# Strassen's rule in the output projection, another product order in the second MLP layer, and operand sums formed earlier

## The chip, the cores and the metric

The kernel runs on one core of one Trainium2 chip. The metric is the device time of one execution in microseconds (us), median of three runs. In this text TensorE multiplies matrices, VectorE (DVE in the profile) and GpSimd (POOL) do elementwise arithmetic, ScalarE (ACT) does activations and copies, and SyncE (SP) starts most transfers. SBUF is the on-chip memory, PSUM the memory that TensorE writes its results to.

## The reference

The input is x, 2 images of 512 channels by 32 x 32 points, in fp32. Two layers follow each other.

The first is a deformable attention block: batch norm, grouped query, offsets from a strided depthwise convolution, keys and values sampled at 64 shifted points, a bias from a small network on all pairs of positions (by far the longest part), softmax, and then the part that this study is about:

```python
out = einsum('bchw,oc->bohw', out, out_w) + out_b     # output projection, 512 x 512
x = x + out
h1 = gelu(einsum(bn2(x), mlp_w1) + mlp_b1)            # MLP, 512 -> 2048
x = x + einsum(h1, mlp_w2) + mlp_b2                   # MLP, 2048 -> 512
```

The second is a full self-attention over the 1024 points of each image, with 512 channels:

```python
attn = softmax((xt @ Wq.T + bq) @ (xt @ Wk.T + bk).T / sqrt(512))
x = x + (attn @ (xt @ Wv.T + bv)) @ Wp.T + bp
```

All products are in fp32.

## The kernel before

**Stages.** The attention bias is computed in 256 slices, up to about 2040 us. Then come, without a barrier, the output projection, the MLP, and the self-attention of image 0 and of image 1. xs holds the running x of both images in SBUF; the projection adds to it, the MLP adds to it, and the self-attention adds to it and stores it.

**Products by Strassen's rule.** Both MLP layers and all of the self-attention multiply 2 x 2 blocks with seven block products in place of eight (the Winograd form, with operand sums that are shared). A block of the moving operand is 128 partitions x 2 x 512. `fold` makes the three weight sums and changes a fourth block in place (four operations, on GpSimd for weights that come from memory). `spread` does the same with the moving operand on VectorE (lines 601, 602, 603 and 605: sums 4 and 5, block 1 in place, sum 6). `PARTS` says which weight block meets which moving block:

```python
PARTS = {1: (0, 0), 2: (1, 2), 3: (6, 3), 4: (2, 6), 5: (4, 4), 6: (5, 5), 7: (3, 1)}
```

So products 1, 2 and 3 need no sum of the moving operand, 5 needs sum 4, 6 needs sum 5, 7 needs block 1 after its change, and 4 needs sum 6. `multiply(pool, order, product, took)` takes the products in a given order: it gets a PSUM tile of two banks, issues four matmuls of 128 x 128 by 512, and calls `took[p]`, which reads the tile on VectorE (`plus`) or ScalarE (copy). In the MLP and the self-attention the PSUM pool mq has four such tiles, so the fifth product waits until the first has been read. In the projection the pool is zp, with three.

**Output projection** (`project(b, h)`, line 657): plain. Four calls, by image and half of the points; in each, four output chunks of four matmuls, 64 matmuls in all. After each chunk VectorE adds it and the bias to xs (line 661). Weights are in vp (already multiplied with the values), the moving operand is qa, the softmax result. The last softmax (`tail`: transpose `pt`, line 533; sums; two transposes `pb`, line 551, that ScalarE copies into qa) runs during image 0's projection and is needed by image 1's.

**MLP.** Eight units: image b, and p of 0 to 3, a quarter of the hidden width. In a unit `layer1` forms a hidden block hm, with GELU on ScalarE (line 690); then `spread(hm)`; then `layer2` multiplies it with the second weights, products in the order 3, 2, 7, 1, 5, 6, 4. Products 2, 3 and 4 are added straight to xs (`give`); 1, 5, 6 and 7 are summed over the four units in acc (`own`), which the last unit adds into xs. `normalise(b)` writes xb, the MLP's input, on ScalarE; `spread(xb)` follows. `load_unit` loads the two weight blocks of the next unit (line 636) and folds them on GpSimd (line 598); there are two buffers of each.

**Self-attention.** `blocks(b)` forms the operand sums of xs on VectorE (tx, lines 793 to 796), and uc is a small sum of a bias. `multiply` then forms the queries (product order 1, 6, 7, 4, 5, 3, 2), the scores, the values and the result.

**What sets the order.** Each engine works through its own queue in order. A tile layer puts in the semaphore waits and fixes each queue's order when the program is built, so an operation can stand elsewhere than in the text. A tile that takes the place of an older one in SBUF or PSUM waits until the older one has been read. The tiles of the MLP's pool mp lie where tiles of the bias stage were.

## Time and profile before

| | |
|---|---|
| time, median of 3 runs | 2813.57 us (2812.54 to 2814.28) |
| span of the profiled execution | 2814.2 us |
| output projection | about 2040.6 to 2098.0 us |
| MLP, eight units | 2098.0 to 2495.6 us |
| self-attention | from 2495.6 us |

The profile gives times within one execution. Its lines of groups and of the timeline read: start (in the timeline), busy us, engine, line of the kernel, operation, output <- inputs, shapes, count, and in brackets the idle time of the engine just before, with what ended it. In the list of stretches each engine has its busy time; the number after the five engines is the TensorE clock that was granted, as a share of full speed. An fp32 matmul of this kernel appears as two records.

### The profile page before, as it was taken

The page shows a single profiled execution, that of the slowest core. Times are in us where ns is not written, and L with a number is a line of the kernel's source. Part 1 is how long each engine was busy: PE and PEld are TensorE (multiplying, and loading weights), DVE is VectorE, ACT ScalarE, POOL GpSimd, SP SyncE. Part 2 cuts the span into 40 slices and gives each one's busy share as a digit, 9 for nine tenths or more (in the row PEclk, how much of TensorE's full clock was granted, in tenths as well). Part 3 has the DMA queues.
Part 4 walks back from the last instruction along what each step waited for, and adds up shares of the span by engine and source line. Part 5 has one row for each costly group of instructions (what it writes and reads, how often), then busy time and mean ns, then how long its engine had stood idle before and what let it go on. Part 6 is the DMA issues. An engine that isn't in the chain of part 4 may idle for free. (4 is left out here: it accounts for less than half of the span.)

```text
span 2814.2 us, 46282 instructions
## 1 busy us (share of the span) xinstructions
PE 2766.7 (98%) x20162; PEld 994.4 (35%) x20162; DVE 2252.5 (80%) x1472; ACT 1562.5 (56%) x1584; POOL 349.7 (12%) x418
## 2 busy tenths in 40 slices
PE   9999999999999999999999999999999999989999
PEld 3332322332233233333333333333344444436455
DVE  5899999899989999899999999999734464365454
ACT  4667667766776677666667667667612031114131
POOL 2111111111110111111111111111132222000000
PEclk9999999999999999999999999999999999999999
DMA  4444344434443444444444444444331101000000
GB/s 166 94 83 99 76 86 89 98 76 83 83 107 68 83 84 83 91 88 86 94 88 86 96 85 91 89 91 83 68 135 45 40 35 45 15 15 1 30 1 30
DMA packets 63530, 210.10 MB, mean 75 GB/s; under 512 B 10976, under 2 KB 13536, under 8 KB 60640
## 3 DMA queue, kind: packets, MB, share of 16 engines
q0 software_dynamic: 36864, 135.28, 25.1%
q1 hardware_dynamic: 25600, 70.79, 8.4%
q8 instruction: 159, 2.61, 0.4%
q10 hardware_dynamic: 864, 1.07, 0.1%
q14 instruction: 43, 0.35, 0.0%
HBM read 67.40 MB, written 6.55 MB: 26 GB/s over the span
## 5 line engine op out<-in xcount | busy, mean ns | idle before, releaser
L480 PE MATMUL ps<-h,cw 128*32 128x512 f32 x16384 | 1798.9, 594 | 15.2 <-ACT rx L486 10.9
L463 DVE CUSTOM_DVE_ANT_1 h<-ta,tb 128x4096 f32<-128x4096 f32 (+1 forms) x257 | 1131.4, 4403 | 77.3 <-PE ps L480 72.1
L480 PEld LDWEIGHTS ps<-h,cw 128*32 128x32 f32 x16384 | 537.2, 110 | 1238.2 <-issue 1163.3
L486 ACT ACTIVATE rx<-ps,sc 128x1024 f32<-128x1024 f32 x512 | 569.3, 1112 | 297.9 <-PE ps L480 293.8
L496 POOL DMA_DIRECT2D ua<-ub x254 | 218.3, 859 | 1738.0 <-DVE ub L494 1603.4
L488 ACT ACTIVATE ua<-ps,sc 128x1024 f32<-128x1024 f32 x256 | 307.8, 1202 | 131.4 <-PE ps L480 131.2
L494 DVE SCALAR_TENSOR_TENSOR ua<-rx,sc,ua 128x1024 f32<-128x1024 f32 x256 | 327.1, 1278 | 53.9 <-ACT ua L488 53.5
L488 ACT ACTIVATE ub<-ps,sc 128x1024 f32<-128x1024 f32 x256 | 307.8, 1203 | 100.6 <-PE ps L480 100.5
L494 DVE SCALAR_TENSOR_TENSOR ub<-rx,sc,ub 128x1024 f32<-128x1024 f32 x256 | 326.9, 1277 | 6.1 <-ACT ub L488 6.1
L681 PE MATMUL sw<-hm,w2t 128*128 128x512 f32 x448 | 195.5, 593 | 11.1 <-DVE hm L603 11.1
L681 PE MATMUL sw<-xb,w1t 128*128 128x512 f32 x448 | 193.7, 592 | 0.8 <-DVE xs L661 0.8
L614 DVE TENSOR_TENSOR hm<-hm,sw 128x1024 f32<-128x1024 f32 x56 | 67.7, 1220 | 119.2 <-PE sw L681 119.2
L517 PE MATMUL sim<-ua,w3s 128*32 128x512 f32 x1024 | 138.6, 599 | 0.4 <-DMA ua<-ub 0.4
L681 PEld LDWEIGHTS sw<-hm,w2t 128*128 128x128 f32 x448 | 84.5, 190 | 120.8 <-issue 120.3
L681 PEld LDWEIGHTS sw<-xb,w1t 128*128 128x128 f32 x448 | 85.0, 190 | 108.3 <-issue 106.4
L690 ACT ACTIVATE hm<-hm,vs 128x512 f32<-128x512 f32 x64 | 42.7, 713 | 130.9 <-DVE hm L614 130.9
L444 ACT ACTIVATE ta<-fb,vs 128x512 f32<-128x512 f32 x64 | 88.7, 1386 | 41.3 <-DVE h L463 30.7
L614 DVE TENSOR_TENSOR xs<-xs,sw 128x1024 f32<-128x1024 f32 (+1 forms) x38 | 43.7, 1160 | 77.7 <-PE sw L681 37.4
L808 PE MATMUL sw<-aT,vt 128*128 128x512 f32 x224 | 96.7, 593 | 0.3 <-ACT aT L888 0.3
L715 ACT COPY hm<-sw 128x1024 f32<-128x1024 f32 x8 | 8.1, 1009 | 148.4 <-PE sw L681 148.4
L598 POOL TENSOR_TENSOR w1t<-w1t 128x512 f32<-128x512 f32 x32 | 58.3, 1842 | 138.1 <-DMA w1t<-in_w 137.3
L808 PEld LDWEIGHTS sw<-aT,vt 128*128 128x128 f32 x224 | 42.4, 190 | 53.4 <-issue 52.6
(189 smaller groups left out, 1445.8 us busy)
## 6 DMA issues: line engine op xcount, KB each, us to landing
ua<-ub POOLq DMA_DIRECT2D x254, 512.0 KB, 4.7
fb<-fdr SPq DMA_DIRECT2D x64, 512.0 KB, 5.0
w1t<-in_w SPq DMA_DIRECT2D x8, 1024.0 KB, 5.0
w2t<-in_w SPq DMA_DIRECT2D x8, 1024.0 KB, 5.4
xn<-in_x SPq DMA_DIRECT2D x8, 512.0 KB, 6.3
xs<-in_x SPq DMA_DIRECT2D x16, 256.0 KB, 6.1
out<-xs SPq DMA_DIRECT2D x16, 256.0 KB, 2.1
wl_s<-in_wl SPq DMA_DIRECT2D x8, 256.0 KB, 4.9
```

What stands on the lines that cost most here:

```text
L444: nc.scalar.activation(ta.rearrange("p j x -> p x j"), fb[:, 0], AF.Identity, bias=col("cb1"), scale=col("w1x"))
L463: nc.vector._custom_dve(TENSOR_ADD_SAT, out=h1[:, y : y + step].rearrange("p y t x -> p (y t x)"), in0=a.unsqueeze(1).to_broadcast([P, ste ...
L480: nc.tensor.matmul(ps[32 * q : 32 * q + 32, h, :], cw2[:, 32 * z : 32 * z + 32], h1[:, 16 * h : 16 * h + 16, q, :], start=True, stop=True,)
L486: nc.scalar.activation(o, ps, AF.Relu, bias=sc[:, 4 + z : 5 + z])
L488: nc.scalar.activation(o, ps, AF.Relu, bias=sc[:, 4 + z : 5 + z], scale=sc[:, z : z + 1])
L494: nc.vector.scalar_tensor_tensor(r[1], r[0], sc[:, z : z + 1], r[1], ALU.mult, ALU.add)
L496: nc.gpsimd.dma_start(out=sums[s][1], in_=sums[s][3], accum_op=ALU.add)
L517: nc.tensor.matmul(sims[gi][q : q + 32, :], w3s[:, 28 - 4 * i : 60 - 4 * i], sums[s + e][z][:, h, :], start=(i == 0), stop=(i == NSL // 2 ...
L598: engine.tensor_tensor(w[o], w[u], w[v], op)
L614: nc.vector.tensor_tensor(out, a, b_, op)
L681: nc.tensor.matmul(ps[:, m, :], w[:, a, k, m * P : (m + 1) * P], x[:, b_, k, :], start=(k == 0), stop=(k == 1),)
L808: nc.tensor.matmul(ps[:, m, :], w[:, a, k, c + m * P : c + (m + 1) * P], x[b_][:, k, :], start=(k == 0), stop=(k == nk - 1),)
```

## The change

Three things change. They leave what is computed the same, up to rounding.

1. The output projection takes Strassen's rule: one call per image, seven products of four matmuls, 56 matmuls in all. The moving operand qa is spread on VectorE and the weights are folded on GpSimd, in place where the rule allows. The sums lie in tiles that later hold xb, acc and a second-layer weight (op0, op1, op2). Because of this `load_unit` of the second unit comes after both calls.
2. The second MLP layer's products come in the order 3, 2, 1, 5, 6, 7, 4, so that product 7, whose operand is the third of the four sums, comes later.
3. `blocks(0)` is called after the sixth unit of the MLP, and uc is formed on GpSimd before the projection. The self-attention then finds its sums ready. For this the sums get homes outside the self-attention's pool (tx with three blocks, t4 in the place of sx), and PSUM tiles share one tag.

```diff
-            ps = pool.tile([P, 2, 512], F32, tag="sw", name="sw")
+            ps = pool.tile([P, 2, 512], F32, tag="ps2", name="sw")
...
+    uc = xq.tile([P, 2], F32, name="uc")
+    nc.gpsimd.tensor_tensor(uc, ub[:, 0, 0:2], ub[:, 0, 2:4], ALU.add)
...
+    def blocks(b):
+        tx = xq.tile([P, 3, 2, 512], F32, name="tx")
+        q = quarters(b)
+        t1, t2, t3 = (tx[:, j] for j in range(3))
+        t4 = f_pool.tile([P, 2, 512], F32, tag="sx", name="t4")
...
-        load_unit(*units[1])
...
-        def project(b, h):
-            n = slice(h * 512, (h + 1) * 512)
-            for o in range(NCH):
-                ps = acc("pso")
-                for k in range(NCH):
-                    nc.tensor.matmul(
-                        ps, vp[:, b * NCH + k, o * P : (o + 1) * P], qa[:, b, k, n],
-                        start=(k == 0), stop=(k == NCH - 1),
+        def project(b, parts, wsum):
+            v, q = vp[:, b * NCH : b * NCH + NCH, :], qa[:, b]
+            w = [v[:, k : k + 2, n : n + 256] for k, n in ((0, 0), (2, 0), (2, 256), (0, 256))]
+            w += [wsum[:, j] for j in range(3)]
+            fold(nc.gpsimd, w)
+            x = [q[:, k : k + 2, n : n + 512] for k in (0, 2) for n in (0, 512)] + [parts[:, j] for j in range(3)]
+            x11, x12, x21, x22 = quarters(b)
+            t = parts[:, 3]
...
+            def first(dst, o, u, op):
+                for m in range(2):
+                    nc.vector.scalar_tensor_tensor(
+                        dst[:, m, :], dst[:, m, :], col("outb", o + m), u[:, m, :], ALU.add, op
                     )
...
+            def o1(ps):
+                nc.scalar.copy(t, ps)
+                first(x11, 0, ps, ALU.add)
...
+            def o5(ps):
+                plus(x22, x22, ps, ALU.subtract)
+                plus(x12, x12, ps)
...
+            def o6(ps):
+                plus(t, t, ps)
+                first(x12, 0, t, ALU.add)
...
+            def o7(ps):
+                plus(t, t, ps)
+                first(x22, 2, t, ALU.subtract)
+                first(x21, 2, t, ALU.subtract)
...
+            spread(x)
+            multiply(zp, (1, 2, 5, 6, 7, 3, 4), go, {
+                1: o1, 2: lambda ps: plus(x11, x11, ps), 5: o5, 6: o6, 7: o7,
+                3: lambda ps: plus(x12, x12, ps), 4: lambda ps: plus(x21, x21, ps, ALU.subtract),
+            })
...
-            multiply(mq, (3, 2, 7, 1, 5, 6, 4), product(w, hm), {
+            multiply(mq, (3, 2, 1, 5, 6, 7, 4), product(w, hm), {
...
-        project(0, 0)
+        op0 = mp.tile([P, 7, 2, 512], F32, tag="xb", name="op0")
+        project(0, op0, op0[:, 4:6].rearrange("p a k n -> p (a k n)")[:, 0:1536].rearrange(
+            "p (a k n) -> p a k n", k=2, n=256
+        ))
         while tail is not None:
             tail = tail if next(tail, 0) is None else None
-        project(0, 1)
         xb = normalise(0)
-        project(1, 0)
+        op1 = mp.tile([P, 4, 2, 512], F32, tag="acc", name="op1")
+        project(1, op1, mp.tile([P, 3, 2, 256], F32, tag="w2t", name="op2", bufs=2))
         spread([xb[:, j] for j in range(7)])
-        project(1, 1)
+        load_unit(*units[1])
...
             layer2(b, p, wb, hm)
+            if i == NU + 1:
+                xbl = blocks(0)
...
-        xbl = blocks(0)
...
-        uc = sp.tile([P, 2], F32, name="uc")
-        nc.vector.tensor_tensor(uc, ub[:, 0, 0:2], ub[:, 0, 2:4], ALU.add)
```

## The prediction

> **What bounds the kernel now.** I read the page's busy shares first, then TensorE's waits from the output projection to the self-attention, then the timeline of the engines there, then the granted clock.

> ```profile
> PE 2766.7 (98%) x20162; PEld 994.4 (35%) x20162; DVE 2252.5 (80%) x1472; ACT 1562.5 (56%) x1584; POOL 349.7 (12%) x418
> ```

> Next is the list of TensorE's waits there: line, releaser, us in total, times, longest.

> ```profile
> PE sw L681 <- DVE hm L603: 11.1, 8, 1.8
> PE sw L808 <- DVE uc L802: 7.6, 1, 7.6
> PE sw L681 <- DVE xs L661: 0.8, 1, 0.8
> ```

> TensorE is busy 98% of the span, so a change is worth the matmuls it removes plus the TensorE waits it removes. After 2040 us there are three waits: once in each of eight MLP units (the third operand sum of a hidden block), once at the start of the self-attention (VectorE sums, then `uc`), once before the MLP. The timeline of TensorE:

> ```profile
> 2122.14 7.03 PE L681 MATMUL sw<-hm,w2t 128*128 128x512 f32 x16
> 2130.81 17.40 PE L681 MATMUL sw<-hm,w2t 128*128 128x512 f32 x40 [1.64 <-DVE hm L603]
> 2148.05 24.20 PE L681 MATMUL sw<-xb,w1t 128*128 128x512 f32 x56
> 2172.08 7.03 PE L681 MATMUL sw<-hm,w2t 128*128 128x512 f32 x16
> ...
> 2495.64 3.60 PE L808 MATMUL sw<-xs,gg 128*128 128x512 f32 x8
> 2506.82 16.54 PE L808 MATMUL sw<-tx,gg 128*128 128x512 f32 x32 [7.58 <-DVE uc L802]
> 2523.19 7.03 PE L808 MATMUL sw<-xs,gg 128*128 128x512 f32 x16
> 2530.06 3.60 PE L808 MATMUL sw<-tx,qs 128*128 128x512 f32 x8
> ```

> A matmul has two records. A layer without a wait takes 2172.08 - 2148.05 = 24.03 us: 0.858 a matmul, 3.43 a Strassen product. In a second layer two products run, then TensorE stands. At the self-attention the 32 records after the wait take 16.54 us where 13.7 are due. The clock tells why (the number after the five engines):

> ```profile
> 2499.60:2501.60 2.00, 0.00 (x0) 0.00 (x0) 2.00 (x3) 1.05 (x2) 0.00 (x0) 1.00 0.00 0
> ...
> 2503.60:2505.60 2.00, 0.00 (x0) 0.00 (x0) 2.00 (x3) 0.00 (x0) 0.00 (x0) 0.50 0.57 149
> ...
> 2507.60:2509.60 2.00, 2.00 (x4) 0.76 (x3) 0.33 (x1) 0.00 (x0) 0.18 (x1) 0.50 0.19 68
> ...
> 2513.60:2515.60 2.00, 2.00 (x6) 0.89 (x5) 1.14 (x1) 0.00 (x0) 0.87 (x1) 1.00 0.01 4
> ```

> The wait cost TensorE half its clock, for some 5 us after it too. Last, VectorE and GpSimd in the first second layer:

> ```profile
> 2127.24 1.22 DVE L602 SCALAR_TENSOR_TENSOR hm<-hm 128x1024 f32<-128x1024 f32 x1
> ...
> 2127.45 7.77 POOL L598 TENSOR_TENSOR w1t<-w1t 128x512 f32<-128x512 f32 x4 [18.77 <-DMA w1t<-in_w]
> ...
> 2128.37 2.29 DVE L603 TENSOR_TENSOR hm<-hm 128x1024 f32<-128x1024 f32 x1
> ...
> 2130.58 2.28 DVE L605 SCALAR_TENSOR_TENSOR hm<-hm 128x1024 f32<-128x1024 f32 x1
> ...
> 2132.79 1.21 DVE L614 TENSOR_TENSOR xs<-xs,sw 128x1024 f32<-128x1024 f32 x1
> ```

> A sum of two SBUF blocks takes 1.22 us alone (a row of them advances by 1.14) and 2.28 beside GpSimd's weight sums, which stretch as well (4 in 7.77 us; 5.06 alone). The sum with a PSUM operand keeps its 1.21.

> [...] 2.28 is near 1.14 plus one GpSimd sum of 1.26. [...]

> **The change, part by part.**

> *Second MLP layer.* Order 3,2,7,1,... becomes 3,2,1,5,6,7,4. Eight units run from 2098.00 to 2495.64, 397.64 us; without waits 8 x 48.06 + 0.1 (the first layer one is longer) = 384.6. The waits are worth 13.0: the listed 11.1 plus the refill after each. Does another wait replace them? From the start of the layer at 2122.14: product 1 starts at +6.9 and needs the last GELU (done +2.8); product 5 at +10.3, first sum (+4.0); product 6 at +13.7, second sum (+6.3) and the PSUM buffer of product 3 (emptied +5.2); product 7 at +17.2, third sum (+8.5) and the buffer of product 2, which VectorE empties behind all four sums, at +11.9. Least slack 5 us. **-13.0.**

> *Self-attention's sums.* The built program puts the four sums of batch 0 on VectorE at the start of the fifth MLP unit, and `uc` on GpSimd early. VectorE is behind there: its MLP tail ends about 6 us after that unit starts, then four sums beside GpSimd's weight sums, 2.4 each. Products 6 and 7 of layer one are then read some 3 us late; their buffers are wanted two products (6.9 us) after they finish, so this is hidden. At the start of self-attention product 6 runs on at once; VectorE is free of the MLP tail 6.4 us after the last MLP product and is wanted at 6.9. From 2495.64 to 2530.06 is 34.42 us, due 24.03: **-10.4** (7.75 of wait, 2.65 of slow clock).

> *Output projection.* Before: 64 matmuls, 54.9 us; after: 2 x 7 products of four, 48.05: -6.9. Against this stand operand sums, 8 GpSimd weight sums and heavier emptying of only three PSUM buffers. I replay it with the queues of the built program[...]. VectorE begins at 2040.75, since the operand tile lies where `ub` was read until then. Its sums, each with a GpSimd sum between, end at 2042.0 (batch 0), 2044.4 (the first of batch 1, queued early), 2046.8, 2049.2, 2051.6; the softmax steps fit in GpSimd's turns. Then follow a reciprocal, half of product 1's sum, a 0.69 us softmax product behind one more GpSimd sum, and the other half, 2054.3. Product 6 wants that PSUM buffer: TensorE, from 2042.01 with three matmuls and products 2 and 5, is there at 2051.45. **Wait 2.9.** Products 6, 7, 3, 4 then run to 2068.1. VectorE's sums for product 7 (four of 0.69, alternating with the sums of the first MLP weights) end at 2070.0. `normalise(0)` writes the tile in which those sums read, so ScalarE starts it only then, and the copy of the last softmax transpose stands behind it until 2071.4; TensorE wants that at 2070.2 for the second transpose: **wait 1.3**. Products 1, 2, 5 of batch 1 end at 2080.5. ScalarE empties product 1 behind eight normalisations (2078.0), VectorE has four sums ahead and finishes at 2082.25: **wait 1.8.** Products 6, 7, 3, 4 end at 2096.05, the last sum at 2097.4, and the MLP starts at 2097.5 against 2098.0. So -6.9 + 6.0 and some transposes and tail: **-0.5.**

> The unknown is the turns. If VectorE never loses one, its chain is 2051.0, there is no first wait, the copy comes in time, and the MLP starts at 2091.6: -6.4. If each two-input operation takes 2.28 and small ones stretch too, product 6 waits 5.5 us: then +2; if that gap halves the clock as at 2502, 2.65 more: about +5. The turn model is in the rows above, so I take -0.5.

> New DMA order: the second unit's second weights come only after product 3 of batch 1 (about 2093) and are wanted past 2160: hidden. The shared PSUM tag and the two homes of the sums add no instructions.

> Sum: 2813.57 - 13.0 - 10.4 - 0.5 = **2789.7 us.**

> **Rivals.** (B) VectorE gets through: 2813.57 - 13.0 - 10.4 - 6.4 = 2783.8. For it: one sum at 2064.57 took only 1.44 beside GpSimd. Against: the three after it took 1.6 to 2.3. (C) The projection becomes bound by VectorE and loses the clock: +5, 2795.2[...]. About the same comes out if a quarter of the second-layer waits and part of the head's wait survive. (D) Slower than before: waits at each product keep TensorE at half clock through the projection, 48 us of matmuls lasting 96 with about 5 of waits: some 44 longer than 57.4, 2813.57 - 23.4 + 44 = 2834. Against it: two products back to back already last 6.9 us, and the clock came back within 5 us at 2511.6.

> **How the numbers follow.** Forecast 0.52, B 0.22, C 0.22, D 0.04. The range runs from B to a little past C, 2783.5 to 2796. Faster 0.94 (A to C, less a little for what I have not seen), same 0.02, slower 0.04.

> **What would show it.** Right: no TensorE wait for operand sums in the MLP, units of 48.1 us; clock 1.00 and no gap after the first product of the self-attention; in the projection TensorE standing before product 6 of batch 0 (some 3 us), before the second transpose, and before product 6 of batch 1; MLP start near 2097.5. Wrong: a wait at product 7 of layer two for a PSUM buffer; a gap in the fifth unit; a clock under 1 in the projection.

## The result, and the profile after

The changed kernel takes 2788.42 us (median of 6 runs, 2783.11 to 2790.0), against 2815.07 for the kernel before in the same session (6 runs, 2812.54 to 2819.63): ratio 0.99, 95% interval 0.9888 to 0.9913. The predicted time was 2789.7, its range 2783.5 to 2796.

First the page's busy shares, then TensorE's waits from the projection to the self-attention (line, releaser, us in total, times, longest), of the changed kernel.

```profile
PE 2752.0 (99%) x20146; PEld 982.0 (35%) x20146; DVE 2283.2 (82%) x1493; ACT 1563.9 (56%) x1586; POOL 367.0 (13%) x427
```

```profile
PE sw L680 <- DVE xs L688: 1.8, 1, 1.8
PE sw L731 <- DVE xs L614: 1.6, 1, 1.6
PE pb L551 <- ACT qa L554: 0.8, 1, 0.8
```

The eight waits for the third operand sum of a hidden block and the 7.6 us for uc are gone. New are a wait in the projection (1.8) and one before the second softmax transpose (0.8); the wait before the MLP has grown from 0.8 to 1.6. TensorE's timeline shows where each stage begins:

```profile
2037.09 1.13 PE L680 MATMUL sw<-qa,vp 128*128 128x512 f32 x2
...
2049.85 3.67 PE L680 MATMUL sw<-op 128*128 128x512 f32 x8 [1.75 <-DVE xs L688]
...
2066.83 0.66 PE L551 MATMUL pb<-kp,sx 128*128 128x128 f32 x4 [0.85 <-ACT qa L554]
...
2091.70 24.30 PE L731 MATMUL sw<-xb,w1t 128*128 128x512 f32 x56 [1.55 <-DVE xs L614]
2115.84 24.20 PE L731 MATMUL sw<-hm,w2t 128*128 128x512 f32 x56
2139.87 24.20 PE L731 MATMUL sw<-xb,w1t 128*128 128x512 f32 x56
...
2476.34 3.60 PE L848 MATMUL sw<-xs,gg 128*128 128x512 f32 x8
2479.77 7.03 PE L848 MATMUL sw<-tx,gg 128*128 128x512 f32 x16
...
2500.37 3.60 PE L848 MATMUL sw<-t,qs 128*128 128x512 f32 x8
```

The second layer of a unit is now one unbroken row of 56 records, 24.03 us from start to start; so is the first layer. At the self-attention the second product follows the first after 3.43 us, and the granted clock there (the number after the five engines) stays at full:

```profile
2478.40:2480.40 2.00, 2.00 (x6) 0.95 (x5) 2.00 (x3) 2.00 (x3) 0.00 (x0) 1.00 0.00 0
```

The differences of those starts, beside the same ones of before:

| stage | before | after | difference | predicted |
|---|---|---|---|---|
| start to projection | 2040.61 | 2037.09 | -3.5 | 0 |
| projection to MLP | 57.39 | 54.61 | -2.8 | -0.5 |
| MLP, eight units | 397.64 | 384.64 | -13.0 | -13.0 |
| self-attention to its eighth product | 34.42 | 24.03 | -10.4 | -10.4 |

They add up to the 29.7 us between the two spans (2814.2 and 2784.5). The first row doesn't belong to the change: the same kernel, profiled again, reached its projection at 2035.03, and kernels that differ only behind it reached it between 2036 and 2041. Medians of several runs even this out and show 26.7.

### The profile page after: what moved, and what is told of

It is laid out like the page before. It is cut to its first block, busy times and chain, and to the rows that moved or that the text cites. A ratio compares the mean times of both kernels' runs of the same rounds, so it can differ in the third digit from the quotient of the medians.

```text
span 2784.5 us, 46289 instructions
## 1 busy us (share of the span) xinstructions
PE 2752.0 (99%) x20146; PEld 982.0 (35%) x20146; DVE 2283.2 (82%) x1493; ACT 1563.9 (56%) x1586; POOL 367.0 (13%) x427
## 4 chain that ended last, share of the span: by engine, by line
PE 84%; DVE 10%; ACT 3%; issue 2%; DMA 1%; SPq 0%; DVEq 0%; POOL 0%; ACTq 0%; POOLq 0%
PE ps L480 53%; PE sw L731 14%; PE sw L848 9%; DVE h L463 4%; PE sim L517 3%; PE sw L946 2%; DVE acc L220 2%; DVE ub L494 1%; DVE ua L494 1%; DVE xs L688 1%; PE pkv L321 1%; ACT rx L486 1%; PE psg L388 1%; DMA xn<-in_x 0%; PE sim L508 0%
## 5 line engine op out<-in xcount | busy, mean ns | idle before, releaser
L480 PEld LDWEIGHTS ps<-h,cw 128*32 128x32 f32 x16384 | 529.4, 110 | 1245.8 <-issue 1167.5
L494 DVE SCALAR_TENSOR_TENSOR ua<-rx,sc,ua 128x1024 f32<-128x1024 f32 x256 | 327.8, 1280 | 53.4 <-ACT ua L488 53.1
L614 DVE TENSOR_TENSOR hm<-hm,sw 128x1024 f32<-128x1024 f32 x56 | 67.6, 1219 | 112.5 <-PE sw L731 112.3
L614 DVE TENSOR_TENSOR xs<-xs,sw 128x1024 f32<-128x1024 f32 (+1 forms) x48 | 55.4, 1170 | 74.0 <-PE sw L848 36.0
L598 POOL TENSOR_TENSOR w1t<-w1t 128x512 f32<-128x512 f32 x32 | 59.6, 1883 | 108.8 <-DMA w1t<-in_w 108.2
L848 PEld LDWEIGHTS sw<-aT,vt 128*128 128x128 f32 x224 | 42.4, 190 | 53.4 <-issue 52.6
```

Of the source, the lines that this page charges most:

```text
L480: nc.tensor.matmul(ps[32 * q : 32 * q + 32, h, :], cw2[:, 32 * z : 32 * z + 32], h1[:, 16 * h : 16 * h + 16, q, :], start=True, stop=True,)
L494: nc.vector.scalar_tensor_tensor(r[1], r[0], sc[:, z : z + 1], r[1], ALU.mult, ALU.add)
L598: engine.tensor_tensor(w[o], w[u], w[v], op)
L614: nc.vector.tensor_tensor(out, a, b_, op)
L848: nc.tensor.matmul(ps[:, m, :], w[:, a, k, c + m * P : c + (m + 1) * P], x[b_][:, k, :], start=(k == 0), stop=(k == nk - 1),)
```

## The experiments

The first four take the parts one by one, each added to the kernel before. The rest vary the projection of the changed kernel, the one term that was off. Runs of one kernel lie up to 7 us apart in the six above (2783.11 to 2790.0) and 11 us in 41 runs of the kernel before (2807.88 to 2819.26), so that differences of a microsecond are read from the traces, as distances from the projection's first matmul.

### The order of the second layer alone

```diff
-            multiply(mq, (3, 2, 7, 1, 5, 6, 4), product(w, hm), {
+            multiply(mq, (3, 2, 1, 5, 6, 7, 4), product(w, hm), {
```

> The kernel before with the second MLP layer's new product order alone. Theory: each of the eight units loses its one TensorE wait (L603's third sum) and nothing takes its place, so units last 48.06 us, the MLP 384.6 us in place of 397.6, and the run is 13.0 us faster than before. Rival (another wait takes its place, the PSUM buffer of product 2 that VectorE empties behind all four sums): a wait at product 7, units above 48.5 us, less than half of the 13 us gained.

2799.38 us, ratio 0.9943 (0.993 to 0.9955): 15.0 us less than the 2814.41 of before. In the trace the MLP runs from 2093.55 to 2478.18, 384.63 us, with no wait for an operand sum and none for a PSUM buffer before product 7. So the order is worth 13.0. It also shortens the wait at the self-attention from 7.58 to 6.39 us, and the stage from 34.42 to 32.99; these 1.4 us overlap with the next part, which removes the whole wait.

### The self-attention's sums alone

```diff
+    uc = xq.tile([P, 2], F32, name="uc")
+    nc.gpsimd.tensor_tensor(uc, ub[:, 0, 0:2], ub[:, 0, 2:4], ALU.add)
...
+            if i == NU + 1:
+                xbl = blocks(0)
...
-        xbl = blocks(0)
```

> The kernel before with blocks(0) and uc formed early alone. Theory: the wait of 7.6 us at the self-attention goes and with it the stretch of half clock, so from the end of the MLP to the scores 34.4 us become 24.0, and the run is 10.4 us faster. The fifth MLP unit shows no gap. Rival (VectorE's backlog in the fifth unit makes TensorE wait there, or only the idle time counts): 7.7 us or less.

2805.63 us, ratio 0.9965 (0.9951 to 0.9978), 8.8 less. The stage takes 24.03 us, 10.4 less. The MLP takes 398.59, 1.0 more: in the fourth unit TensorE waits 2.75 us where it waited 1.79, since there the second sum too (L602, 2.17 us) fell beside GpSimd's weight sums. The net of the trace is -9.4.

### The projection alone

```diff
-            ps = pool.tile([P, 2, 512], F32, tag="sw", name="sw")
+            ps = pool.tile([P, 2, 512], F32, tag="ps2", name="sw")
...
-        def project(b, h):
...
+        def project(b, parts, wsum):
...
+            multiply(zp, (1, 2, 5, 6, 7, 3, 4), go, {
...
+        load_unit(*units[1])
```

> The changed kernel with the old product order of the second layer and the old place of blocks(0) and uc: the Strassen projection alone. Theory: 6.9 us of matmuls go, waits before product 6 of image 0 (about 1.8), before the second softmax transpose (about 0.8) and at the start of the MLP (about 1.6, 0.8 before) come, so it is 2 to 3.5 us faster than before. Rival (the projection gives its full 6.9 us, or nothing): outside that.

2812.5 us over 21 runs, ratio 0.9989 (0.9983 to 0.9996). The projection runs from 2038.04 to 2092.62, 54.58 us: -2.8, with the waits of the changed kernel (1.73, 0.84 and 1.55). But in the profiled run the MLP takes 400.39 us in place of 397.64 and gives all of it back. TensorE in the fourth unit, and two neighbouring stretches with its clock:

```profile
2276.45 19.10 PE L728 MATMUL sw<-hm,w2t 128*128 128x512 f32 x40 [2.85 <-DVE hm L603]
```

```profile
2273.73:2277.14 3.41, 0.69 (x2) 0.48 (x3) 3.41 (x3) 0.03 (x1) 3.41 (x2) 1.00 0.00 0
2277.14:2280.55 3.41, 3.41 (x5) 1.36 (x5) 3.41 (x3) 0.87 (x1) 2.50 (x2) 0.50 0.00 0
```

The wait is 2.85 us in place of 1.79, and the 40 records after it take 19.10 us in place of 17.40, a part of them at half clock (granted 0.50). GpSimd's weight sums began at 2271.75 here, VectorE's L602 at 2271.83, and L602, L603 and L605 took 2.28 us each; in the kernel before GpSimd began 0.06 us after L602, which kept its 1.22. The measured gain of 1.9 us (1.1 to 4.8 by the interval) lies just under the expected 2 to 3.5, between the 2.8 of the stage and the nothing of this one trace. The trace shows how the old order can lose the projection's gain; whether the other runs lost it there too is not shown. The new order has room for such a shift.

### A filled wait

To part the wait at the self-attention from what it does to the clock, eight matmuls whose result nobody reads go behind the first product of the kernel before.

```diff
             def q1(ps):
+                if b == 0:
+                    pf = mq.tile([P, 2, 512], F32, tag="sw", name="pf")
+                    for _ in range(8):
+                        nc.tensor.matmul(
+                            pf[:, 0, :], gg[:, 0, 0, 0:P], xs[:, 0, 0, 0:512], start=True, stop=True
+                        )
```

> The kernel before with eight matmuls whose result nobody reads, put on TensorE behind the first product of image 0's queries, where it stood idle; nothing of the computation is left out. Theory (idle TensorE loses its clock): product 6 starts as late as before, but the granted clock stays at 1.00, the four products after it take 13.7 us and not 16.5, and the run is about 2.6 us faster though it does more work. Rival (the clock after the wait has another cause, or the slow records are the profile's model): no gain, or a loss.

2812.06 us over 21 runs, ratio 0.9992 (0.9985 to 0.9998): more work and 2.35 us less. TensorE:

```profile
2496.75 7.03 PE L822 MATMUL pf<-xs,gg 128*128 128x512 f32 x16
2504.49 13.97 PE L808 MATMUL sw<-tx,gg 128*128 128x512 f32 x32 [0.71 <-DVE uc L802]
```

The same 32 records take 13.97 us in place of 16.54 once TensorE is kept busy, and the stage 31.85 in place of 34.42. So some 2.6 of the predicted 10.4 were slow clock (granted 0.50 from 2501.75 to 2511.99 in the trace of before), and not waiting.

### Order and sums with the plain projection

The changed kernel with the plain projection of before (the second layer's order and the self-attention's sums as in the first two diffs).

> The kernel before with the new product order and the early sums, and the plain projection. Theory (the three parts add up and the projection is worth 2.8 us in the changed kernel, from its start to the MLP 54.6 against 57.4 us): 23 to 24 us faster than before, 2.8 slower than the changed kernel. Rival (the projection's worth was spent elsewhere, as in the run with the projection alone, where the fourth MLP unit gave it back): the same time as the changed kernel.

2791.89 us, ratio 0.9913 (0.99 to 0.9927), 24.1 less than 2815.97. Projection 57.40 us, MLP 384.63, self-attention stage 24.04. So -13.0 and -10.4 add up, and Strassen's rule in the projection is worth the other 2.8 us.

### The projection's weight sums left out

```diff
-            w += [wsum[:, j] for j in range(3)]
-            fold(nc.gpsimd, w)
+            w += w[0:3]
```

> The changed kernel without the eight weight sums of the projection on GpSimd; weight blocks stand in for the sums, so the projection's result is left wrong, all else is done as before. Theory[...]: VectorE's sums of 1024 drop from 1.7 to 1.2 us, its half of product 1's sum comes about 2 us earlier, and the wait of 1.75 us before product 6 of image 0 falls under 0.4. Rival (three PSUM buffers alone set that wait): it stays above 1.2 us.

2787.49 us, ratio 0.9902 (0.9889 to 0.9916). VectorE's sums take 1.21 us each and the wait before product 6 of image 0 is gone, so GpSimd's weight sums, beside which they took 1.69, had made it. But TensorE then stands before product 6 of image 1:

```profile
2077.43 3.67 PE L679 MATMUL sw<-op,vp 128*128 128x512 f32 x8 [2.18 <-DVE xs L687]
```

GpSimd starts the MLP's weight sums earlier here, and all three of image 1's sums take 2.3 us. The projection takes 54.59 us, as in the changed kernel: the wait has moved, and nothing was won.

### Two rearrangements that miss

In the first, VectorE reads product 1 from ScalarE's copy and not from PSUM, so that the buffer comes free without VectorE.

```diff
                 nc.scalar.copy(t, ps)
-                first(x11, 0, ps, ALU.add)
+                first(x11, 0, t, ALU.add)
```

> The changed kernel, but the sum of product 1 reads ScalarE's copy t and not PSUM, so that ScalarE alone gives the buffer back. Theory (PSUM buffer of product 1 behind VectorE's queue makes the first wait, but VectorE's chain to the normalisation stays as long): the wait before product 6 of image 0 goes, the wait before the second softmax transpose grows from 0.85 to about 2.5 us, and the time is the same within 0.5 us. Rival (the first wait is worth its 1.75 us): 1.7 us faster than the changed kernel.

2789.67 us, ratio 0.9908 (0.9894 to 0.9921); projection 56.26, 1.65 more than the changed kernel. Product 6 doesn't wait any more; product 7 does, for the buffer of product 2, and it then runs in part at half clock (granted 0.50 from 2058 to 2060):

```profile
2057.66 5.35 PE L680 MATMUL sw<-qa,vp 128*128 128x512 f32 x8 [2.33 <-DVE xs L614]
```

The two bias sums of product 1 now take both inputs from SBUF. Beside GpSimd they took 1.63 and 1.75 us, where they had taken 0.69 and 0.73 from PSUM, and so VectorE empties product 2 late. The expected growth of the wait before the second softmax transpose didn't come (0.83 us, expected about 2.5).

The second keeps this and also moves the projection's sums of image 0 out of xb's place, so that normalise needn't wait for product 7, and puts the last softmax transposes later (sent[5] is the last matmul of the sixth product).

```diff
...
-        op0 = mp.tile([P, 7, 2, 512], F32, tag="xb", name="op0")
...
+        op0 = mp.tile([P, 4, 2, 512], F32, tag="acc", name="op0")
...
+        project(0, op0, mp.tile([P, 3, 2, 256], F32, tag="w1t", name="os0", bufs=2))
...
+        with tc.issue_after(sent[5]):
+            while tail is not None:
+                tail = tail if next(tail, 0) is None else None
```

> As the run before, and the projection's operand sums of image 0 lie in acc's tile and a first-layer weight's, so that the normalisation need not wait for them, with the last softmax transposes held behind product 3. Theory: both waits of image 0 go, the projection takes 54.6 - 2.6 = about 52 us, and the kernel is 2 to 3 us faster than the changed one. Rival (the sums of image 1, which now need the tile of image 0, come late and make a wait before product 5 or 6 of image 1): no gain.

2791.34 us, ratio 0.9914 (0.9901 to 0.9928); projection 58.25, 3.6 more. ScalarE now starts normalising early, but the fifth operation waits for VectorE's sum of product 3, and the copy of the first transpose stands behind it in ScalarE's queue: TensorE waits 5.21 us for that copy before the second transpose.

### What bounds the projection: three steps

The wait moves, but not at random. Product 6 of image 1 begins 39.1 us after the projection's start in the changed kernel and again 39.1 with the weight sums left out. That points at one chain on VectorE, up to the emptying of image 1's product 1, and at GpSimd, beside which image 1's sums took 2.3 us in place of 1.21. Three kernels try this.

First, products 1 and 2 of image 0 swapped, so that the buffer for the fourth product needs one VectorE operation and not two with a softmax step between.

```diff
-            multiply(zp, (1, 2, 5, 6, 7, 3, 4), go, {
+            multiply(zp, (2, 1, 5, 6, 7, 3, 4) if b == 0 else (1, 2, 5, 6, 7, 3, 4), go, {
```

> The changed kernel with products 1 and 2 of image 0's projection swapped (2, 1, 5, 6, 7, 3, 4); nothing else. The fourth product needs the PSUM buffer of the first. Product 1 is emptied by two bias operations with a softmax step between them, ready 2049.8 after a start at 2037.1; product 2 by one sum of 1.21 us, which VectorE can begin as soon as its four operand sums and the reciprocal are through, 2047.4. Theory that the wait is for that one buffer: the wait before product 6 falls from 1.75 to about 0.5, no other wait grows, the projection takes 53.4 us in place of 54.6, the time falls by about 1.2 us. Rival, that VectorE's whole load up to the softmax copy is the bound: the wait reappears later (product 7, the second softmax transposition or image 1), projection within 0.4 us of 54.6, no change in time.

> The changed kernel itself, unaltered, in the same call as the swapped order, so that the two can be compared on one chip: projection 54.6 us with a wait of 1.75 us before product 6, ratio to the kernel before 0.990 to 0.991 by either theory.

2786.28 us for the swap and 2785.67 for the unaltered kernel on the same chip (ratios 0.9879 and 0.9878, intervals 0.9859 to 0.9899 and 0.9859 to 0.9897). TensorE of the swapped kernel:

```profile
2049.68 3.67 PE L680 MATMUL sw<-op 128*128 128x512 f32 x8 [0.63 <-DVE xs L614]
...
2077.12 3.67 PE L680 MATMUL sw<-op,op 128*128 128x512 f32 x8 [1.18 <-DVE xs L688]
```

The first wait shrinks by 1.1 us, as worked out, and all of it comes back before product 6 of image 1, which again begins 39.1 us after the start; the projection takes 54.59. The rival of that expectation holds. The traces show where the gain went. Image 1's three operand sums began 33.1 us after the start in the changed kernel, 32.0 here and 30.9 with the weight sums left out; one, two and all three of them met GpSimd's weight sums and took 2.3 us in place of 1.21. Each start 1.1 us earlier was paid back by one more lost turn.

Second, the swap, and image 1's weight sums in two places, so that both weights of the second unit arrive later and GpSimd has nothing to do beside image 1's operand sums.

```diff
-            w += [wsum[:, j] for j in range(3)]
+            w += wsum
...
-        project(1, op1, mp.tile([P, 3, 2, 256], F32, tag="w2t", name="op2", bufs=2))
+        op2 = mp.tile([P, 2, 2, 256], F32, tag="w1t", name="op2", bufs=2)
+        op3 = mp.tile([P, 1, 2, 256], F32, tag="w2t", name="op3", bufs=2)
+        project(1, op1, [op2[:, 0], op2[:, 1], op3[:, 0]])
...
```

> The swapped order (2, 1, 5, 6, 7, 3, 4 for image 0), and the three weight sums of image 1 in two places: two in a first-layer weight buffer, one in a second-layer one, so that both weights of the second unit arrive only after product 6 and product 3 of image 1 and GpSimd's sums of them no longer lie beside VectorE's operand sums of image 1. Every queue keeps its order. Theory, that VectorE's chain up to the emptying of image 1's product 1 (39.1 us after the start in three kernels) is the bound, lengthened by two lost turns of 1.08 us: the operand sums take 1.2 us each, that chain ends near 36.9, TensorE arrives at 37.9 and does not wait before image 1's product 6, the projection takes about 53.4 us in place of 54.6 and the MLP stays at 384.6. Rival, that the bound is elsewhere (the copies of the softmax transpose, ScalarE's normalisations): the wait of 1.2 us stays, projection 54.6. Second rival: the later weights make the second unit wait, MLP above 385. In time at most 1.2 us, near what five rounds can tell.

2789.3 us, ratio 0.9906 (0.9889 to 0.9922). The three sums take 1.22 us each and product 6 of image 1 no longer waits, as the theory says. But GpSimd's sums now start at 2084.05 and meet the emptying of product 7. VectorE there, and TensorE at the start of the MLP:

```profile
2085.06 5.83 DVE L688 SCALAR_TENSOR_TENSOR xs<-xs,vs,op 128x512 f32<-128x512 f32 x4
```

```profile
2093.20 26.00 PE L731 MATMUL sw<-xb,w1t 128*128 128x512 f32 x56 [3.91 <-DVE xs L614]
```

The last emptying comes late, TensorE waits 3.91 us, and the first layer takes 26.00 us in place of 24.30, a part of it at half clock (granted 0.50 from 2094 to 2096); the MLP as a whole takes 386.33. Projection 55.5 us, where 53.4 were expected.

Third, the swap, and image 1's sum of products 1, 6 and 7 (t) in the place of a first-layer weight, so that the second unit's weights come only after its last use.

```diff
-        def project(b, parts, wsum):
+        def project(b, parts, wsum, t):
...
-            t = parts[:, 3]
...
-        project(1, op1, mp.tile([P, 3, 2, 256], F32, tag="w2t", name="op2", bufs=2))
+        project(1, op1, mp.tile([P, 3, 2, 256], F32, tag="w2t", name="op2", bufs=2),
+                mp.tile([P, 2, 512], F32, tag="w1t", name="op3", bufs=2))
...
```

> The swapped order (2, 1, 5, 6, 7, 3, 4 for image 0), and image 1's sum of products 1, 6 and 7 (t) in the place of the second unit's first-layer weight, its three weight sums in that of the second-layer weight as in the changed kernel. Both weights of the second unit then arrive only after product 3 of image 1 and after the last use of t, and GpSimd stands still through all of image 1's two-input work on VectorE, its operand sums and the emptying of product 7. Theory, that VectorE's lost turns set the end of the projection wherever they fall: no wait before product 6 of image 1 and, unlike when the weights came earlier, a wait of at most 1.6 us before the MLP with the clock at 1; projection 53.4 us in place of 54.6, MLP 384.6 to 384.8. Rival, that the end is set by the number of VectorE's operations and not by turns: MLP start wait over 3 us again, projection 54.6 or more. In time some 1.2 us under the changed kernel, which five rounds can hardly tell; the trace decides.

2787.17 us, ratio 0.9896 (0.9879 to 0.9912). TensorE, then VectorE:

```profile
2037.04 1.13 PE L679 MATMUL sw<-qa,vp 128*128 128x512 f32 x2
...
2071.32 7.03 PE L679 MATMUL sw<-op,op 128*128 128x512 f32 x16
...
2089.97 24.30 PE L730 MATMUL sw<-xb,w1t 128*128 128x512 f32 x56 [1.31 <-DVE xs L614]
```

```profile
2084.41 2.74 DVE L687 SCALAR_TENSOR_TENSOR xs<-xs,vs,op 128x512 f32<-128x512 f32 x4
```

The same four operations take 2.74 us without GpSimd and 5.83 beside it. The projection takes 52.93 us, 1.7 less than the changed kernel, and the MLP still 384.63. The total doesn't show it: 1.7 us are within what its runs differ by, and no claim of a faster kernel is made from the times. Of the three steps, the first removed the wait that it aimed at, but its rival held; the second removed the next wait and won no time; the third came out as expected (52.93 us, where 53.4 were expected). Each of these readings rests on one trace.

## Why the prediction was right, by its own steps

The sum came closer than its parts. It was counted from 2813.57 us, and the kernel before took 2815.07 over six runs, so that a gain of 23.9 us was forecast and 26.7 came. Most of the missing 2.8 is the projection. That the time still lies within 1.3 us of the forecast is in part luck.

*Second MLP layer, -13.0.* Right in mechanism and size: 384.64 us against 384.6, no wait at product 7, the order alone 384.63. The least slack in the prediction's own list is 4.1 us (product 1 and the last GELU) and not 5; nothing came of it.

*Self-attention's sums, -10.4.* Right: 24.03 us against 24.03, and the fifth unit shows no gap. The split into 7.75 of wait and 2.65 of clock is confirmed by the filled wait (2.57 us off the stage). What the prediction missed is that the order alone takes 1.4 of this; the sum isn't touched by it, since the wait goes entirely. Two details were off without effect: VectorE's tail of the MLP ended 9.8 us after the fifth unit began and not about 6, and only one of the four sums lost a turn (2.28 us, the others 1.21).

*Output projection, -0.5.* The mechanism is right, the size is not: -2.8. This is the mis-sized term. The matmuls saved are the predicted 6.9. The three waits were put at 2.9, 1.3 and 1.8 us, 6.0 in all. The profile lists 1.75 and 0.85 for the first two, and the third is hidden in a row that takes 7.38 us in place of 7.03. Counted from start to start, which takes in what a wait costs the matmuls beside it, they cost 2.0, 1.0 and 0.35, 3.4 in all. The wait before the MLP grew by 0.7, where 0.4 had been allowed for transposes and tail. So -6.9 + 3.4 + 0.7 is the measured -2.8. The turns were overrated. VectorE in the changed kernel:

```profile
2041.27 1.68 DVE L602 SCALAR_TENSOR_TENSOR op<-op,qa 128x1024 f32<-128x1024 f32 x1
2042.87 0.68 DVE L538 TENSOR_TENSOR sx<-pt,mx 128x512 f32<-128x512 f32 x1
2043.47 1.69 DVE L603 TENSOR_TENSOR qa<-qa 128x1024 f32<-128x1024 f32 x1
```

A sum and the softmax step after it together take 2.2 us, the time of one GpSimd sum beside them (2.25), so the step costs nothing, as predicted; but I took 2.4 a turn, an estimate from the rows of before (1.14 + 1.26). The sums end 10.3 us after the start and not 11.0, the buffer of product 1 is free at 12.6 and not 13.7, and TensorE is there at 10.8, as predicted. For image 1 GpSimd was done 34.3 us after the start, so that two of its three sums took 1.21 us, and VectorE released product 6 at 38.9 and not 41.6. Who begins first matters too, as far as two traces show it: in the fourth MLP unit L602 took 2.28 us where GpSimd had begun 0.08 us before it (projection alone), and 1.22 where it had begun 0.06 us before GpSimd (kernel before).

*Rivals.* B (-6.4, no turns lost) and C (+5, turns and half clock) didn't come, but later kernels moved towards both: the last rearrangement, with GpSimd out of the way for image 1, has a projection of 52.93, -4.5 against before; the moved tiles have 58.25, +0.9. The copy read by VectorE, the moved tiles and the later weights each lost the clock for a stretch: 0.50 was granted in the first and the last, and in the moved tiles 14 records took 7.50 us after the wait of 5.21, where the 14 of image 0 took 6.17. D, a projection at half clock throughout, came in no run.

## What to carry to other kernels

A VectorE sum of two SBUF blocks that stands beside GpSimd's weight sums is costed by turns (2.28 us here, 1.22 alone): lay out both queues, and let what keeps its time beside GpSimd (here a sum with a PSUM operand, 1.21 us) fit inside the other's turn. Where a removed wait comes back later, compare the time at which the next release happens, counted from the stage's start: a figure that stays the same in several kernels (39.1 us here) says that something between takes the gain back, and the traces then have to show what. Here it was turns lost to GpSimd. And give the latest operand of a product chain the latest place in it; here that one line brought about half of the whole gain (13.0 of 26.2 us by the stages).

## What the runs showed of the hardware

```profile
2274.08:2277.49 3.41, 2.29 (x6) 0.75 (x4) 3.41 (x3) 2.45 (x4) 2.99 (x2) 1.00 0.00 0
2277.49:2280.90 3.41, 1.78 (x4) 0.87 (x5) 3.41 (x2) 0.00 (x0) 3.41 (x3) 1.00 0.00 0
```

The waits of 2.33 us (2.31 in one interval) and 2.18 us (split, 0.47 and 1.70) fit it too. Full clock came back only after an interval with at most 0.28 us of idle time. No run moved one and the same wait across the grid to test this.

An eviction from PSUM with one SBUF operand of 1024 columns took 1.21 to 1.22 us beside GpSimd in the kernels before and after, as without it, while the two-input SBUF operation of 512 columns went from 0.69 to 1.46 us, the mean of four that took 5.83 us together (2.74 without GpSimd). In this kernel the last ones of a stage are thus a costly place for GpSimd's work: the wait before the MLP was 3.91 us with it there and 1.31 without.
